# A graph layer's gathers and place transfers get semaphores of their own, one-hots are made two groups at a time, and five more groups leave the GpSimd queue

## The chip, the cores and the metric

The kernel runs on one core of one Trainium2 chip. The metric is the device time of one execution in microseconds (us); the lower the better. A kernel's time is the median of several executions. Engines are named as the profile names them: PE is TensorE, PEld its weight loads, DVE is VectorE, ACT is ScalarE, POOL is GpSimd, SP is SyncE. A name with a q behind it (DVEq, SPq, POOLq) is what the engine's instruction queue does beside its arithmetic: it waits for semaphores, loads registers and issues DMAs.

## What is computed

One layer of message passing on a graph of 12,500 nodes (128 numbers each) and 400,000 edges (32 numbers each), sorted by destination:

```python
h = relu(layernorm(x))
m = relu(concat(h[src], h[dst], edge_attr) @ w1 + b1) @ w2 + b2
agg = segment_sum(m, dst, 12500)
gi, gh = agg @ w_ih + b_ih, h @ w_hh + b_hh
r, z = sigmoid(i_r + h_r), sigmoid(i_z + h_z)
n = tanh(i_n + r * h_n)
out = x + (1 - z) * n + z * h
```

All of it is float32.

## The kernel before

**Once at the start.** The kernel normalizes the nodes, keeps h transposed in SBUF (`hT_all`), and writes A = h @ w1[0:128] to memory in HBM, one row of 512 bytes per node. The part for the destinations, B = h @ w1[128:256] + b1, is made in batches. Then the edges are worked through.

**Groups and units.** The 3125 tiles of 128 edges are cut into 391 groups `k` of 8 tiles (1024 edges; group 0 has 5 tiles). A group is two units `u` = 2k and 2k+1. Since the edges are sorted, a group touches at most 32 neighbouring nodes in each of its two halves.

**Work on a group.** For each group:

- `fetch` (L556) brings, for two groups at once, the destinations of the edges and the edge attributes into a buffer `L` with two DMAs on SP's queue, L563 and L566. There are three such buffers.
- `onehot_T` (L568, instruction at L575) turns the destinations in `L` into a one-hot matrix on VectorE, in place. With the rows of B in `RW` (`window_rows`, L602, SP) TensorE makes from it and from the attributes the part of the first product that doesn't depend on the source node (`pre`, L673).
- The row A[src] of every edge has to be added to that. There are four ways, and the dictionary `SPREAD` (L56) says how many groups go which way. **By GpSimd**: `gather` (L148) issues an indirect DMA per tile, eight per group (L156), into one of 11 buffers `G`; the first nine groups take raw rows of x, since A isn't there yet. **By SyncE**: 1024 single DMAs of 512 bytes each (L952) into `G_sp`. **By ScalarE or VectorE**: 1024 columns of `hT_all` are copied, one per edge, into a tile `HE_act` (L960) or, two edges an instruction, `HE_dve` (L967, put in order by L972); TensorE then multiplies them with w1[0:128] (L684).
- Where rows came by DMA, `add` adds them to `pre` and takes the relu in one instruction on VectorE (L701), into `RB`. For groups copied by ScalarE or VectorE the relu is one on ScalarE (L710).
- `onehot` (L606, instruction at L623) makes on VectorE a one-hot of the destinations with edges on the partitions, 128 by 256 per group, in one of six buffers `OH`. TensorE multiplies it with `RB` and sums up by node (`seg`, L724, after a zeroing product at L719).
- Each block of 14 groups ends in a `node` step: gates, tanh, output.

**Groups made by hand.** `one_by_one` (L934) is the work of ScalarE, VectorE and SyncE on such groups. The numbers of the rows are loaded from the tile `at` into registers of the engine (L945): 16 at a time on ScalarE, 32 on VectorE and SyncE. `run_jobs` (L988) strews the copies evenly over the units ahead of the group, in four phases of each unit. ScalarE starts on its first one at unit 4, VectorE at unit 14, SyncE at unit 24 (`START`), and each goes from one to the next.

**Order.** All instructions stand in the order in which the program writes them (`manual_schedule`), each engine has its own queue, and semaphores between them are set by the framework. A DMA counts up one of eight shared semaphores of its kind (one set for the hardware queue that SP uses, one for GpSimd's), by turns. An instruction that reads what eight DMAs brought waits for each of the eight, and a DMA whose turn falls on a semaphore waits until the DMA before it on that semaphore has landed. At unit `u` the loop runs `gathers(u)`, at even units `window_rows(k + 4)` and, every other group, `fetch`; then `stages(u)`: `onehot_T` or `onehot` for three groups ahead, `pre` three units ahead, `add` two units ahead; then `seg(u)`.

Of the kernel before, what the change touches and what calls it, by code (L numbers as in the profile page):

```python
# [9 lines left out]
F32 = mybir.dt.float32  # L10
F16 = mybir.dt.float16
I32 = mybir.dt.int32
# [17 lines left out]
V = 32  # L30
# [9 lines left out]
QP = 2  # L40
# [4 lines left out]
RAW = 9  # L45
GBUFS = 11
# [17 lines left out]
def tile_gnn(ctx: ExitStack, tc: tile.TileContext, x, src, srcT, dstT, dstP, eaT, eaP, w1, b1, w2T, b2,  # L64
             wih, bih, whh, bhh, out):
    nc = tc.nc
    ctx.enter_context(tc.manual_schedule())
    const = ctx.enter_context(tc.tile_pool(name="const", bufs=1))
# [12 lines left out]
    def tiles(k):  # L81
        return (0 if k == 0 else SUP0 + (k - 1) * PAIR, SUP0 + k * PAIR)


    def unit_tiles(u):
        k, h = divmod(u, 2)
        t0, t1 = tiles(k)
        return [(t0 + a * GRP + j, j, a) for j in (2 * h, 2 * h + 1) for a in range(2)
                if t0 + a * GRP + j < t1]

    mode, order = {}, {m: [] for m in SPREAD}
    for m, n in SPREAD.items():
# [49 lines left out]
    taker, ring = {}, []  # L142
    for k in range(NP):
        if k not in mode:
            taker[k] = ring[-GBUFS] if len(ring) >= GBUFS else -1
            ring.append(k)

    def gather(k):  # L148
        if k >= NP or k in mode:
            return  # L150
        G[k] = gp.tile([128, GRP, 2, D], F32, name="G")
        table = x if k < RAW else A
        for u in (2 * k, 2 * k + 1):
            for t, j, a in unit_tiles(u):
                c, i = divmod(t, CH)
                nc.gpsimd.indirect_dma_start(  # L156
                    out=G[k][:, j, a, :], out_offset=None, in_=table,
                    in_offset=bass.IndirectOffsetOnAxis(ap=src_i[c][:, i:i + 1], axis=0))

    for k in range(RAW):  # L160
        gather(k)
# [181 lines left out]
    with tc.tile_pool(name="pp", bufs=3) as pp:  # L343
# [50 lines left out]
        row = lambda v: v.rearrange("(o f) -> o f", o=1)  # L394
# [34 lines left out]
        for q in range(NC + 3):  # L429
            if q < NC:  # L430
                b, i0, c, e, P, n0 = chunk(q)
# [3 lines left out]
            if 1 <= q <= NC:  # L435
                b, i0, c, e, P, n0 = chunk(q - 1)
# [6 lines left out]
            if q >= 3:  # L443
                b, i0, c, e, P, n0 = chunk(q - 3)
# [3 lines left out]
            if q < NC:  # L448
                b, i0, c, e, P, n0 = chunk(q)
# [4 lines left out]
            if 1 <= q <= NC:  # L454
                b, i0, c, e, P, n0 = chunk(q - 1)
# [31 lines left out]
    dlast = p3.tile([128, BLOCKS[-1][1] + 128], F16, name="dlast", bufs=1)  # L487
# [63 lines left out]


    Ls, OH, RT, HE, SEG = ({} for _ in range(5))
    hand = {}

    def fetch(q):  # L556
        if q * QP >= NP:
            return
        n = min(QP, NP - q * QP)
        c = slice(q * QP * 512, (q * QP + n) * 512)  # L560
        Ls[q] = p3.tile([128, QP * 512], F32, name="L")
        p = dstP[:, c]
        nc.sync.dma_start(  # L563
            Ls[q].bitcast(I32)[:2 * V, :n * 512],
            bass.AP(tensor=p.tensor, offset=p.offset, ap=[list(p.ap[0]), [0, V], [1, n * 512]]))
        nc.sync.dma_start(Ls[q][2 * V:, :n * 512], eaP[:, c])  # L566

    def onehot_T(k):  # L568
        if k >= NP:
            return  # L570
        c = slice((k % QP) * 512, (k % QP + 1) * 512)
        o, i = Ls[k // QP][:2 * V, c], Ls[k // QP].bitcast(I32)[:2 * V, c]
        n = k - BLOCKS[-1][0]
        if n < 0:
            nc.vector.tensor_scalar(o, i, node_of[:, k:k + 1], None, op0=ALU.is_equal)  # L575
        else:
            nc.vector.tensor_scalar(o, i, node_of[:, k:k + 1], 0.0, op0=ALU.is_equal, op1=ALU.add,
                                    accum_out=dlast[:2 * V, n:n + 1])


    bases = {}
# [22 lines left out]
                                  "(p f) -> p f", p=V))  # L604

    def onehot(k):  # L606
        if k >= NP:
            return
        t0, t1 = tiles(k)
        OH[k] = OHB[k % len(OHB)]  # L610
        row = SEGB[((k - 3) // 2 + 1) % 2][:, 256:256 + V]
        for a in range(2) if k == 0 else (None,):
            if a is None:
                o, s = OH[k].rearrange("p j a v -> p a j v"), slice(t0, t1)
                d = dloc[:, s].rearrange("p (a j) -> p a j", a=2)[:, :, :, None]
                shape = [128, 2, GRP, V]
                i = row[:, None, None, :]
            else:
                e = min(t1, (a + 1) * GRP)
                o, d = OH[k][:, :e - a * GRP, a, :], dloc[:, a * GRP:e, None]  # L620
                shape = [128, e - a * GRP, V]
                i = row[:, None, :]
            nc.vector.tensor_tensor(o, d.to_broadcast(shape), i.to_broadcast(shape),  # L623
                                    op=ALU.is_equal)

    def unit(u):
        k, h = divmod(u, 2)
# [59 lines left out]
    def add(u):  # L687
        if u >= NU or u < 0:
            return
        k, h = divmod(u, 2)  # L690
        if h == 0 and k < NP - 1:
            return
        c = slice(0, PAIR) if k < NP - 1 else slice(GRP * h, GRP * h + GRP)
        o, p = RB[k % 2][:, c, :D], PP[k][:, c, :]
        if u in HE or k in hand:
            RT[u] = o, p
            HE.pop(u, None)
            HE.pop(u - 1, None)
            hand.pop(k, None)
        else:  # L700
            nc.vector._custom_dve(TENSOR_ADD_SAT, out=o, in0=p,  # L701
                                  in1=G[k].rearrange("p j a f -> p (j a) f")[:, c, :], s0=float("inf"), s1=0.0)
        if h == 1:
            PP.pop(k)
            G.pop(k, None)
# [9 lines left out]
    def seg(u):  # L715
        k, h = divmod(u, 2)
        p = SEGB[(k // 2) % 2]
        if h == 0 and k % 2 == 0:
            nc.tensor.matmul(p[:, :D + 1], zrow[:, :128], zrow[:, :D + 1], start=True, stop=False)  # L719
        l = unit_tiles(u)  # L720
        rest = l if h else l + unit_tiles(u + 1)
        for i, (t, j, a) in enumerate(l):
            r0 = 2 * V * (k % 2) + V * a
            nc.tensor.matmul(p[r0:r0 + V, :D + 1], OH[k][:, j, a, :],  # L724
                             RB[k % 2][:, 2 * j + a, :D + 1], start=False,
                             stop=all(b != a for _, _, b in rest[i + 1:]))

# [287 lines left out]
    for q in range(3):  # L1015
        fetch(q)
# [4 lines left out]
    def stages(u):  # L1021
        if u + 7 >= 0:
            raw_stats(u + 7)
        if u + 6 >= 0:
            raw_fin(u + 6)
            raw_h(u + 6)
        if u % 2 == 0:
            onehot_T(u // 2 + 3)
        elif u > -7:
            onehot(u // 2 + 3)  # L1030
        if u + 4 >= 0:
            raw_turn(u + 4)
        if u + 3 >= 0:
            pre(u + 3)
        if u + 2 >= 0:
            add(u + 2)
            relu(u + 2)
# [18 lines left out]
    for u in range(NU):  # L1056
        k, h = divmod(u, 2)
        gathers(u)
        if h == 0:
            window_rows(k + 4)  # L1060
            if k % QP == 0:
                fetch(k // QP + 3)
            if k and k == BLOCKS[block(k)][0]:
                nodes_left.append([node(block(k) - 1), 2 if k < BLOCKS[-1][0] else 1])
            if k % PLACE == 1:
                indices(k // PLACE + 2)
            if k % PLACE == 5:
# [23 lines left out]
        other(1)  # L1091
        other(2)
        seg(u)
        if u == 0:
            node_setup()
# [106 lines left out]
    f = nc.values_load(flag[0:1, 0:1], min_val=0, max_val=1)  # L1202
# [67 lines left out]
```

## Time and profile before

| | |
|---|---|
| time, median of 3 runs | 3404.46 us (3404.36 to 3407.26) |
| profiled execution, its own time | 3403.76 us |
| its span, first to last instruction | 3401.8 us |
| busy: PE / PEld / DVE | 71% / 46% / 65% |
| busy: ACT / POOL | 91% / 75% |
| granted TensorE clock, mean | 0.796 |
| mean DMA rate | 99 GB/s |
| groups gathered by POOL / by hand on ACT, DVE, SP | 334 / 28, 27, 2 |

The busy time counts arithmetic, and for POOL the making of indirect DMAs. Loading registers, waiting for semaphores and issuing DMAs is not counted as busy. "Idle before" a group of instructions is the idle time of the engine just ahead of them, with what ended it; "issue" means that nothing which the profile shows was waited for.

### The profile page before, as it was taken

What the parts mean: (1) busy time and instruction counts of PE and PEld (TensorE: products, weight loads), DVE (VectorE), ACT (ScalarE), POOL (GpSimd) and SP (SyncE); (2) the same over time, 40 slices, a digit from 0 to 9 for tenths busy, and PEclk for the clock granted to TensorE, in tenths of its full rate; (3) what the DMA queues carried; (4) which work ended last, traced back from release to release, by engine and by line L of the source; (5) the groups of instructions that cost most, each with busy time, mean ns of one, the idle gap of its engine ahead of it and who ended that gap; (6) DMA issues with size and microseconds to landing.
All of it is one profiled execution on the core that took longest, in us unless ns stands there. A gap on an engine that the chain in (4) does not pass through costs nothing. (4 is left out here: it accounts for less than half of the span.)

```text
span 3401.8 us, 88642 instructions
## 1 busy us (share of the span) xinstructions
PE 2417.4 (71%) x13113; PEld 1563.7 (46%) x13113; DVE 2225.1 (65%) x16468; ACT 3079.4 (91%) x29057; POOL 2566.1 (75%) x2678
## 2 busy tenths in 40 slices
PE   7567777777677767776777667676677767766767
PEld 7444444444445444544444444444444434444445
DVE  8556666666676666666666666666666666666665
ACT  7699999999999998999899988988988898898984
POOL 7777777777777777777777777777777777777776
PEclk9777887887887778777877877788777778777878
DMA  6434444434443333343434433443433334343332
GB/s 213 106 88 93 97 100 99 101 94 100 102 98 94 98 99 95 95 101 97 98 93 99 98 94 93 96 96 93 98 93 92 95 94 99 92 97 96 92 92 73
DMA packets 191316, 335.44 MB, mean 99 GB/s; under 512 B 66753, under 2 KB 112384, under 8 KB 190729
## 3 DMA queue, kind: packets, MB, share of 16 engines
q0 software_dynamic: 85408, 175.09, 23.0%
q1 hardware_dynamic: 105177, 154.58, 16.4%
q14 instruction: 478, 3.92, 0.4%
q8 instruction: 109, 1.79, 0.2%
q10 hardware_dynamic: 144, 0.07, 0.0%
HBM read 309.24 MB, written 20.24 MB: 97 GB/s over the span
## 5 line engine op out<-in xcount | busy, mean ns | idle before, releaser
L156 POOL DMA_INDIRECT G<-A,src_i x2600 | 2498.9, 961 | 796.2 <-issue 753.7
L960 ACT COPY HE_act<-hT_all 128x4 uint8 x28672 | 2886.8, 189 | 51.4 <-issue 27.0
L967 DVE SCALAR_TENSOR_TENSOR both<-hT_all 128x4 uint16 x13824 | 1173.4, 153 | 988.5 <-issue 980.7
L673 PE MATMUL pre<-RW,L 128*128 128x256 f32 x3128 | 1132.4, 488 | 229.8 <-DVE RB L701 220.6
L673 PEld LDWEIGHTS pre<-RW,L 128*128 128x128 f32 x3128 | 660.6, 236 | 506.1 <-DVE RB L701 234.0
L724 PE MATMUL seg<-RB,OH 128*32 128x129 f32 x6250 | 603.9, 324 | 380.0 <-DVE RB L701 349.7
L724 PEld LDWEIGHTS seg<-RB,OH 128*32 128x32 f32 x6250 | 333.1, 125 | 820.4 <-DVE RB L701 532.7
L701 DVE CUSTOM_DVE_ANT_0 RB<-pre,G 128x1024 f32<-128x1024 f32 (+1 forms) x326 | 394.5, 1210 | 62.7 <-DMA G<-A,src_i 49.2
L575 DVE TENSOR_SCALAR L<-L,node_of 64x512 f32<-64x512 int32 x382 | 186.7, 489 | 9.7 <-DMA L<-in_dstP 9.4
L719 PE MATMUL seg<-zrow 1*128 1x129 bf16 x196 | 45.3, 231 | 164.4 <-DVE OH L623 164.2
L623 DVE TENSOR_TENSOR OH<-dloc,seg 128x256 f32<-128x256 f16 (+1 forms) x392 | 159.5, 407 | 0.5 <-issue 0.5
L750 PE MATMUL nd<-spot,sums 128*128 128x40 f32 x782 | 116.6, 321 | 1.2 <-DVE sums L733 1.2
L750 PEld LDWEIGHTS nd<-spot,sums 128*128 128x128 f32 x782 | 112.4, 231 | 10.5 <-issue 9.0
L710 ACT ACTIVATE RB<-pre 128x1024 f32<-128x1024 f32 x64 | 65.0, 1015 | 52.4 <-PE pre L684 52.4
L809 ACT ACTIVATE gt<-nd 128x512 f32<-128x512 f32 (+2 forms) x28 | 16.4, 585 | 96.5 <-PE nd L803 96.5
L972 DVE COPY HE_dve<-both 128x512 uint8<-128x512 uint8 x216 | 96.6, 447 | 7.4
L684 PEld LDWEIGHTS pre<-w1a,HE_act 128*128 128x128 f32 x448 | 88.4, 245 | 11.6
L684 PEld LDWEIGHTS pre<-w1a,HE_dve 128*128 128x128 f32 x432 | 87.9, 252 | 12.1
L684 PE MATMUL pre<-w1a,HE_act 128*128 128x128 f32 x448 | 86.4, 327 | 0.0
L684 PE MATMUL pre<-w1a,HE_dve 128*128 128x128 f32 x432 | 85.1, 333 | 0.0
L156 POOL DMA_INDIRECT G<-in_x,src_i x69 | 65.9, 954 | 21.8 <-issue 20.7
L233 PE MATMUL nd<-w1b,hT_all 128*128 128x128 f32 x224 | 45.5, 346 | 43.3 <-DVE xb L835 43.3
(177 smaller groups left out, 1383.9 us busy)
## 6 DMA issues: line engine op xcount, KB each, us to landing
L<-in_dstP SPq DMA_DIRECT2D x195, 256.0 KB
L<-in_eaP SPq DMA_DIRECT2D x195, 256.0 KB
G<-A,src_i POOLq DMA_INDIRECT x2600
G_sp<-A SPq DMA_DIRECT2D x2048, 0.5 KB
RW<-B SPq DMA_DIRECT2D x782, 16.0 KB
xb<-in_x SPq DMA_DIRECT2D x26, 256.0 KB
out<-xb SPq DMA_DIRECT2D x26, 256.0 KB
xs<-in_x SPq DMA_DIRECT2D x11, 512.0 KB
```

The source lines that it names most:

```text
L156: nc.gpsimd.indirect_dma_start(out=G[k][:, j, a, :], out_offset=None, in_=table, in_offset=bass.IndirectOffsetOnAxis(ap=src_i[c][:, i:i + ...
L575: nc.vector.tensor_scalar(o, i, node_of[:, k:k + 1], None, op0=ALU.is_equal)
L623: nc.vector.tensor_tensor(o, d.to_broadcast(shape), i.to_broadcast(shape), op=ALU.is_equal)
L673: nc.tensor.matmul(p[:, 2 * i:2 * i + 2, :], Ls[k // QP][:, c0:c0 + 128], RW[k % 4], start=True, stop=not raw)
L684: nc.tensor.matmul(p[:, 2 * i + a, :], cols, w1a, start=False, stop=n + 1 == len(l) or l[n + 1][1] != j)
L701: nc.vector._custom_dve(TENSOR_ADD_SAT, out=o, in0=p, in1=G[k].rearrange("p j a f -> p (j a) f")[:, c, :], s0=float("inf"), s1=0.0)
L710: nc.scalar.activation(o, p, AF.Relu)
L724: nc.tensor.matmul(p[r0:r0 + V, :D + 1], OH[k][:, j, a, :], RB[k % 2][:, 2 * j + a, :D + 1], start=False, stop=all(b != a for _, _, b in r ...
L750: nc.tensor.matmul(p[:, bass.ds(offs[i], V + SHIFT)], sums[:, slot(b, i), :D], spot[:, i % 2, :], start=False, stop=i == len(offs) - 1)
L960: nc.scalar.copy(he[:, e * 4:e * 4 + 4], column(v))
L967: nc.vector.scalar_tensor_tensor(both[:, (e0 % PIECE + i) // 2, :], column(vals[i + 1]), 256.0, column(vals[i]), op0=ALU.mult, op1=ALU.add)
L972: nc.vector.tensor_copy(he[:, p0 * 4:(p0 + PIECE) * 4].rearrange("p (n c b) -> p n c b", c=2, b=4), both.bitcast(U8).rearrange("p n (b c) ...
```

## The change

The change has four parts.

1. **Gathers.** Eleven semaphores `filled`, one per buffer `G`. All gathers but those of the first nine groups and of the last one count up the semaphore of their buffer and take no turn on the shared ones. Ahead of the `add` stands one wait until all eight have landed.
2. **Places.** Three semaphores `landed`, one per buffer `L`. The two DMAs of `fetch` count up that of their buffer, and take no turn on the shared ones. VectorE waits for it once per buffer, ahead of the first `onehot_T`.
3. **One-hots.** `onehot` makes those of an even group and the one behind it in a single instruction, 128 by 512, in one of three buffers of double size. Groups 0 and 1 and the last stay single. The elements lie in the order of the tiles, half by half, and `seg` reads them so.
4. **Spread.** ScalarE 28 to 29 groups, VectorE 27 to 28, SyncE 2 to 5; so GpSimd gathers 329 and not 334.

```diff
-SPREAD = {"dve": 27, "act": 28, "sp": 2}
+SPREAD = {"dve": 28, "act": 29, "sp": 5}
...
+    filled = [tc.alloc_semaphore(f"filled{i}") for i in range(GBUFS)]
+    uses, goal = [0] * GBUFS, {}
     def gather(k):
...
+        i = ring.index(k) % GBUFS
+        if RAW <= k < NP - 1:
+            uses[i] += 1
+            goal[k] = filled[i], 16 * PAIR * uses[i]
...
-                nc.gpsimd.indirect_dma_start(
+                fetched = nc.gpsimd.indirect_dma_start(
...
+                if k in goal:
+                    fetched.then_inc(goal[k][0], 16)
+                    tc.no_tile_sem_insts.add(fetched.ins.name)
+                    tc.add_to_no_dep_group(f"rows{k}", fetched.ins)
...
-    OHB = [const.tile([128, GRP, 2, V], F32, name=f"OH{i}") for i in range(6)]
+    OHB = [const.tile([128, 2 * PAIR, V], F32, name=f"OH{i}") for i in range(3)]
...
+    landed = [tc.alloc_semaphore(f"landed{i}") for i in range(3)]
...
+            fetched.then_inc(landed[q % 3], 16)
+            tc.no_tile_sem_insts.add(fetched.ins.name)
+            tc.add_to_no_dep_group(f"places{q}", fetched.ins)
...
+        q = k // QP
+        if k % QP == 0:
+            nc.vector.wait_ge(landed[q % 3], 32 * (q // 3 + 1))
...
-        if k >= NP:
+        if k >= NP or (k % 2 and k > 1):
             return
+        o = OHB[(k // 2) % len(OHB)]
+        n = 2 if 1 < k < NP - 1 else 1
+        t0, t1 = tiles(k)[0], tiles(k + n - 1)[1]
...
+            nc.vector.tensor_tensor(p, dloc[:, e0:e1, None].to_broadcast(shape),
+                                    row[:, None, :].to_broadcast(shape), op=ALU.is_equal)
...
+            if k in goal:
+                nc.vector.wait_ge(*goal[k])
```

More of the change, by code (lines that the diff above doesn't have):

```diff
@@ L562, in fetch @@
         p = dstP[:, c]
[L563 to L566, printed above, removed]
+        for fetched in (
+                nc.sync.dma_start(
+                    Ls[q].bitcast(I32)[:2 * V, :n * 512],
+                    bass.AP(tensor=p.tensor, offset=p.offset, ap=[list(p.ap[0]), [0, V], [1, n * 512]])),
+                nc.sync.dma_start(Ls[q][2 * V:, :n * 512], eaP[:, c])):
+            fetched.then_inc(landed[q % 3], 16)
+            tc.no_tile_sem_insts.add(fetched.ins.name)
+            tc.add_to_no_dep_group(f"places{q}", fetched.ins)
     def onehot_T(k):
@@ L574, in onehot_T @@
         if n < 0:
-            nc.vector.tensor_scalar(o, i, node_of[:, k:k + 1], None, op0=ALU.is_equal)
+            made = nc.vector.tensor_scalar(o, i, node_of[:, k:k + 1], None, op0=ALU.is_equal)
         else:
-            nc.vector.tensor_scalar(o, i, node_of[:, k:k + 1], 0.0, op0=ALU.is_equal, op1=ALU.add,
-                                    accum_out=dlast[:2 * V, n:n + 1])
+            made = nc.vector.tensor_scalar(o, i, node_of[:, k:k + 1], 0.0, op0=ALU.is_equal, op1=ALU.add,
+                                           accum_out=dlast[:2 * V, n:n + 1])
+        tc.declare_no_dep(made.ins, group=f"places{q}", reason="behind the wait for the landing")
+        if k % QP == 0:
+            tc.declare_fence(made.ins, group=f"places{q}")
     bases = {}
@@ L606, in onehot @@
     def onehot(k):
-        if k >= NP:
+        if k >= NP or (k % 2 and k > 1):
             return
-        t0, t1 = tiles(k)
-        OH[k] = OHB[k % len(OHB)]
+        o = OHB[(k // 2) % len(OHB)]
         row = SEGB[((k - 3) // 2 + 1) % 2][:, 256:256 + V]
[L612 to L624, printed above, removed]
+        n = 2 if 1 < k < NP - 1 else 1
+        for i in range(n):
+            OH[k + i] = o[:, PAIR * ((k + i) % 2):PAIR * ((k + i) % 2) + PAIR, :]
+        t0, t1 = tiles(k)[0], tiles(k + n - 1)[1]
+        if k:
+            parts = ((o[:, PAIR * (k % 2):PAIR * (k % 2) + t1 - t0, :], t0, t1),)
+        else:
+            parts = tuple((OH[0][:, a * GRP:min(t1, (a + 1) * GRP), :], a * GRP, min(t1, (a + 1) * GRP))
+                          for a in range(2))
+        for p, e0, e1 in parts:
+            shape = [128, e1 - e0, V]
+            nc.vector.tensor_tensor(p, dloc[:, e0:e1, None].to_broadcast(shape),
+                                    row[:, None, :].to_broadcast(shape), op=ALU.is_equal)
     def unit(u):
@@ L700, in add @@
         else:
-            nc.vector._custom_dve(TENSOR_ADD_SAT, out=o, in0=p,
+            if k in goal:
+                nc.vector.wait_ge(*goal[k])
+            made = nc.vector._custom_dve(TENSOR_ADD_SAT, out=o, in0=p,
                                   in1=G[k].rearrange("p j a f -> p (j a) f")[:, c, :], s0=float("inf"), s1=0.0)
+            if k in goal:
+                tc.declare_no_dep(made.ins, group=f"rows{k}", reason="behind the wait for the landing")
+                tc.declare_fence(made.ins, group=f"rows{k}")
         if h == 1:
@@ L723, in seg @@
             r0 = 2 * V * (k % 2) + V * a
-            nc.tensor.matmul(p[r0:r0 + V, :D + 1], OH[k][:, j, a, :],
+            nc.tensor.matmul(p[r0:r0 + V, :D + 1], OH[k][:, a * GRP + j, :],
                              RB[k % 2][:, 2 * j + a, :D + 1], start=False,
```

## The prediction

> **What bounds the kernel now.** The page comes first: its span, and what POOL does.
>
> ```profile
> span 3401.8 us, 88642 instructions
> L156 POOL DMA_INDIRECT G<-A,src_i x2600 | 2498.9, 961 | 796.2 <-issue 753.7
> L156 POOL DMA_INDIRECT G<-in_x,src_i x69 | 65.9, 954 | 21.8 <-issue 20.7
> ```
>
> POOL is called 75% busy, but the two rows with the idle time before them make 2498.9 + 796.2 + 65.9 + 21.8 = 3382.8 us of a span of 3401.8. So a gather takes 3382.8 / 2669 = 1.267 us, pause included. The timeline of POOL, first and last rows, says what the pause is:
>
> ```profile
> 3.27 1.10 POOL L156 DMA_INDIRECT G<-in_x,src_i  x1 [1.10 <-DMA src_i<-in_srcT]
> 4.67 0.94 POOL L156 DMA_INDIRECT G<-in_x,src_i  x1 [0.31 <-issue]
> 5.92 0.94 POOL L156 DMA_INDIRECT G<-in_x,src_i  x1 [0.30 <-issue]
> ...
> 3382.70 0.94 POOL L156 DMA_INDIRECT G<-A,src_i  x1 [0.30 <-issue]
> 3383.95 0.94 POOL L156 DMA_INDIRECT G<-A,src_i  x1 [0.30 <-issue]
> ```
>
> The same 0.30 us stands before the second gather, whose shared semaphore no DMA has used yet, and before the last. It belongs to the instruction; no semaphore is waited for in it. POOL works without a hole from 3.27 to 3384.89, and 16.9 us later all is over.
>
> That isn't the whole bound. Next I counted gathers (first pair of rows) and adds (second pair) before and after 250 us, with the stretches' view held to L156 and to L701:
>
> ```profile
> 0.00:250.00 250.00, 185.24 (x194) 0.82 0.49 137
> 250.00:1600.00 1350.00, 1024.05 (x1066) 0.81 0.40 98
> ...
> 0.00:250.00 250.00, 7.27 (x6) 0.82 0.49 137
> 250.00:1600.00 1350.00, 172.19 (x142) 0.81 0.40 98
> ```
>
> At 250 us POOL has issued 194 gathers, 24.6 groups. Nine of them (raw rows) need no add, six are added: it leads by 9.6 groups, with 11 buffers. At 1600 us it is 157.9 groups, nine raw, 148 added: a lead of 0.9. So for half of the run VectorE catches up, and is itself the bound; from then on it meets POOL. The waits of VectorE in 250 to 1600, in 1700 to 3350 and over all (in this order) say the same:
>
> ```profile
> DVE both L967 <- issue: 413.5, 368, 2.6
> DVE RB L701 <- DMA G<-A,src_i: 1.3, 4, 0.6
> ...
> DVE RB L701 <- DMA G<-A,src_i: 38.1, 23, 3.7
> DVE xb L238 <- PE nd L233: 16.6, 4, 4.8
> DVE RB L701 <- PE pre L673: 8.7, 4, 2.9
> ...
> DVE both L967 <- issue: 980.7, 847, 2.8
> DVE RB L701 <- DMA G<-A,src_i: 49.2, 31, 3.7
> ```
>
> In the first stretch VectorE waits for nobody: the stretches' view has it busy for 915.91 of 1350 us, and 413.5 are "issue".
>
> ```profile
> 250.00:1600.00 1350.00, 993.62 (x5380) 631.28 (x5379) 915.91 (x6957) 1290.30 (x12575) 1024.05 (x1066) 0.81 0.40 98
> 1700.00:3350.00 1650.00, 1145.71 (x6180) 726.58 (x6181) 1058.83 (x7993) 1498.79 (x14423) 1252.55 (x1305) 0.78 0.39 95
> ```
>
> Three engines lie close together, then. **POOL** sets the end; **VectorE** would end at most 49.2 us sooner without the waits for gathers, 3352.6, and at least 3327.3 if a late VectorE met the 16.6 + 8.7 us of waits on PE no more. I take the middle, 3340. **ScalarE** (fourth figure) has 59.7 us idle in the first stretch and 151.2 in the second.
>
> **The change part by part.** *Gathers off POOL.* Five groups of eight at 1.267 us are 50.7 us. What is left per gather stays as it is, since the pause held no wait. POOL would end at 3334.2, and with the same 16.9 us of tail the span is 3351.1. That is the floor.
>
> *One more group on VectorE.* The groups by line of VectorE in 250 to 1600, with the one-hot and the nearest 128x512 instruction that also reads PSUM:
>
> ```profile
> L967 DVE SCALAR_TENSOR_TENSOR both<-hT_all 128x4 uint16 x6116 | 519.2, 153 | 419.7 <-issue 413.5 <-DMA G_sp<-A 5.2
> L701 DVE CUSTOM_DVE_ANT_0 RB<-pre,G 128x1024 f32<-128x1024 f32 x142 | 172.2, 1213 | 4.7 <-PE pre L673 2.9 <-DMA G<-A,src_i 1.3 <-issue 0.4
> L623 DVE TENSOR_TENSOR OH<-dloc,seg 128x256 f32<-128x256 f16 x166 | 67.8, 408 | 0.0
> L972 DVE COPY HE_dve<-both 128x512 uint8<-128x512 uint8 x96 | 43.1, 449 | 3.3
> L813 DVE TENSOR_TENSOR gt<-gt,misc 128x512 f32<-128x512 f32 x12 | 8.2, 680 | 0.1
> ```
>
> A group is 512 instructions of L967 at (519.2 + 413.5) / 6116 = 0.1525 us, 78.1, and eight copies of L972 at 0.449, 3.6: together 81.7 us more. Adds go from 328 to 326, 2.4 less; SyncE's three new groups are added as the gathered ones were.
>
> *One-hots.* 195 pairs become one instruction each. By the durations, two of 408 ns against one of about 680 save 0.136 us a pair. But such instructions overlap:
>
> ```profile
> 1518.67 0.41 DVE L623 TENSOR_TENSOR OH<-dloc,seg 128x256 f32<-128x256 f16 x1
> 1519.01 1.21 DVE L701 CUSTOM_DVE_ANT_0 RB<-pre,G 128x1024 f32<-128x1024 f32 x1
> ```
>
> The next one starts 0.34 us after the one-hot. So I count 0.34 twice against 0.68 - 0.07 = 0.61, about 0.07 a pair: 14 us less. The ends are 0 (512 elements cost two times 256) and 26.5.
>
> *Waits of VectorE.* What a line's own view lists on the queue:
>
> ```profile
> L701 DVEq EVENT_SEMAPHORE  x1358: 21/50/2846, 201.2 to 3386.5; - x194
> L575 DVEq EVENT_SEMAPHORE  x129: 21/21/21, 148.2 to 3301.6; - x129
> L945 DVEq TENSOR_LOAD <-at x864: 2095/2150/3239, 188.2 to 3336.5; - x173
> ```
>
> An add has about four waiting instructions ahead of it for its eight shared semaphores, 50 ns each (median). One per gathered group stays, so some 1010 go: 50.5 us of queue time. The waits of L575 grow from 129 to about 196, 1.4 us. Is queue time VectorE's time? The queue is served in order, and the load of 32 numbers (2.15 us) comes behind the waits. Of 864 loads, 847 end with VectorE idle ("issue", 847 times), so there the queue is the later one, and what stands ahead of the load counts. Where it has instructions enough queued, a wait is hidden. The ends are 0 and twice 50.5, if the pause behind a wait is as long as the wait (an estimate; no row shows it). I take 50.5.
>
> [...]
>
> VectorE's own end: 3340 + 81.7 - 2.4 - 14 - 50.5 + 1.4 = 3356.2. That is 5 us behind POOL's floor, and the later one counts.
>
> *ScalarE.* One more group; its groups by line in 250 to 1600:
>
> ```profile
> L960 ACT COPY HE_act<-hT_all 128x4 uint8 x12514 | 1251.7, 189 | 18.9 <-issue 8.5
> L710 ACT ACTIVATE RB<-pre 128x1024 f32<-128x1024 f32 x24 | 24.4, 1016 | 15.1 <-PE pre L684 15.1
> L809 ACT ACTIVATE gt<-nd 128x512 f32<-128x512 f32 x12 | 7.1, 592 | 21.8 <-PE nd L803 21.8
> ```
>
> 1024 copies at 0.100 us and two more relus at 1.0 are 104.4 us, over 3200 us 3.3%. It had 59.7 / 1350 = 4.4% idle where VectorE was the bound. So it just fits, hidden in idle time that it spent on PE's results. [...]
>
> *SyncE's queue.* Its waits, and rows of its timeline:
>
> ```profile
> SPq L952 <- DMA L<-in_dstP: 865.4, 150, 8.1
> SPq L563 <- PE pre L673: 233.9, 63, 14.1
> ...
> 1521.30 1.27 SPq L952 DMA_DIRECT2D G_sp<-A  x4
> 1522.74 0.81 SPq L602 DMA_DIRECT2D RW<-B  x2
> 1523.67 0.60 SPq L563 DMA_DIRECT2D L<-in_dstP  x1
> 1524.32 0.50 SPq L566 DMA_DIRECT2D L<-in_eaP  x1
> ```
>
> Before, single rows waited 865.4 us for transfers of places that held their shared semaphore; that goes. A single row costs 1.27 / 4 = 0.32 us, a group with its 32 loads (at 2.15, as VectorE's) 396, five 1980. The 782 transfers of L602 at 0.41 and 196 pairs of places at 1.15 add 546. In all 2526 of 3350: it fits, and the waits for PE (233.9) are room too. What is queued behind such rows are the next places and `RW`; places are asked for six groups ahead.
>
> *One-hots are made up to a group earlier, with the same memory.* That takes a buffer one group sooner from `seg`; PE, 71% busy, is the engine that waits for VectorE, so I count nothing. PE gets 16 more products at L684: nothing either, by the same cover.
>
> **The sum.** The later of 3351.1 and 3356.2, and the 2.0 us that the profiled execution lies over its span (3403.76 - 3401.8): 3358. That execution is 0.7 us under the median of the runs, which I leave aside.
>
> **The rivals.**
>
> *ScalarE binds.* If half of its idle 4.4% can't be filled, because gates wait for PE whenever they come, it lacks 3.3 + 2.2 - 4.4 = 1.1% of 3200, 35 us over POOL's floor: 3351 + 35 + 2 = 3388. For it: 91% busy. Against it: its idle time lies before L710 and L809, and a later ScalarE finds those results there.
>
> [...]
>
> *VectorE keeps up easily.* The waits save twice as much, POOL decides alone: 3353. For it: the pause behind waits.
>
> *The change doesn't do what it says:* gathers still wait on something shared, or SyncE falls behind with five groups and VectorE waits for rows instead. Then what POOL saves is lost again: about 3404.
>
> **Chances.** Forecast with POOL's floor in it, 3350 to 3375: 0.56. ScalarE or VectorE somewhat late, 3375 to 3397: 0.17. No change (waits hidden with the middle value, or lost again), within 0.2% of 3404, about what a measurement of this kernel can tell from no change: 0.07. Slower: 0.14. Below 3350, if a gather itself becomes cheaper than 1.267: 0.06. So faster 0.79, same 0.07, slower 0.14. The range is 3347 to 3405; what it leaves out is the slower cases and half of the last.
>
> **What would show it.** POOL without holes, 40 gathers fewer, 1.267 us each, ending near 3334: right for the first step. Semaphore instructions of L701's line down to about 350, and the time of L967 with its "issue" per instruction below 0.1525 us: right for the waits; unchanged: the waits were hidden. One-hots near 680 ns, 195 fewer. VectorE's waits for gathers shrink below 49.2 us if it is the bound, and grow if it keeps up. Waits of SP on places gone. The forecast fails if POOL shows waits for buffers (`RB` from VectorE), which means that VectorE fell back, or if ScalarE's idle time is gone and PE waits for it.

## The result, and the profile after

The changed kernel takes 4152.09 us (median of 4 runs, 4145.63 to 4160.77), against 3405.17 (4 runs, 3404.36 to 3407.26) for the kernel before beside it: 1.2196 times as long, 95% interval 1.2181 to 1.221. It is **22% slower**, and the forecast was 3358 with a range up to 3405.

The page of the changed kernel, its span and the groups that answer to those of before (GpSimd's gathers, TensorE's first product, VectorE's one-hots and pair copies):

```profile
span 4158.9 us, 94794 instructions
...
L163 POOL DMA_INDIRECT G<-A,src_i x2560 | 2453.2, 958 | 1508.9 <-DVE RB L724 766.8
...
L694 PE MATMUL pre<-RW,L 128*128 128x256 f32 x3128 | 1230.5, 523 | 1400.5 <-DMA RW<-B 1243.0
L993 DVE SCALAR_TENSOR_TENSOR both<-hT_all 128x4 uint16 x14336 | 1210.4, 156 | 1066.0 <-issue 1052.0
...
L594 DVE TENSOR_SCALAR L<-L,node_of 64x512 f32<-64x512 int32 x382 | 189.0, 495 | 679.1 <-DMA L<-in_eaP 679.1
...
L644 DVE TENSOR_TENSOR OH<-dloc,seg 128x512 f32<-128x512 f16 (+1 forms) x198 | 133.2, 673 | 0.0
```

Read the last column. The instructions are hardly dearer: a gather is 958 ns (961 before), a pair copy 156 ns (153). Among the rows shown only TensorE's first product takes clearly longer, 523 ns where it took 488, at a mean granted clock of 0.748 where it was 0.796. But every engine waits. TensorE waits 1243.0 us for `RW`, VectorE 679.1 us for the places, GpSimd 766.8 us for buffers that VectorE's adds give back. (GpSimd's wait for `RB` is the sign by which the prediction said that it would fail.) The first two are waits for DMAs, and both of those are issued by **SyncE**. So its queue is the place to look. What SyncE waits for (us in all, times, longest):

```profile
SPq L978 <- DMA G_sp<-A: 886.7, 172, 8.2
SPq L576 <- PE pre L694: 68.7, 28, 12.6
SPq L624 <- PE pre L694: 60.6, 16, 12.2
```

Before, the same kind of wait was 865.4 us under the name of the places; now it is 886.7 under the name of the single rows themselves. The name changed with the semaphore's other user, the time didn't. And SyncE waits little for TensorE to free the buffers of places (68.7 us at this line, 233.9 before): it is seldom early. The timeline of SyncE late in the run shows the wait itself:

```profile
4002.96 0.61 SPq L576 DMA_DIRECT2D L<-in_dstP  x1
4003.63 0.50 SPq L579 DMA_DIRECT2D L<-in_eaP  x1
4004.24 13.20 SPq L978 DMA_DIRECT2D G_sp<-A  x16
4017.53 0.82 SPq L624 DMA_DIRECT2D RW<-B  x2
4018.45 5.08 SPq L978 DMA_DIRECT2D G_sp<-A  x16
4023.78 0.41 SPq L865 DMA_DIRECT2D out<-xb  x1
4024.35 0.82 SPq L624 DMA_DIRECT2D RW<-B  x2
4025.22 0.59 SPq L576 DMA_DIRECT2D L<-in_dstP  x1
```

Sixteen rows cost 5.08 us (0.32 each) where nothing large is ahead, and 13.20 us right behind the two transfers of places, 512 KB in all. Taken from the trace row by row, the 13.20 us hold the rows themselves (5.2 us), a register load that falls among them (2.2), one stop of 5.3 us ahead of the ninth row, and a shorter one behind the load. The first eight rows find the eight shared semaphores free; the ninth has to wait until the row eight back has landed. By the semaphores' counts in the trace those eight rows land 7.0 to 8.0 us after their issue. Over the run the first eight rows behind places take 7.9 us to land (median), all others 1.4; and 172 of the 175 stops of over 0.5 us ahead of a row stand ahead of the ninth row behind a transfer of places. The waits for rows last 5.2 us on average (886.7 / 172), and one comes with nearly every transfer of places, that is, once per two groups. Behind it on the same queue stand `RW` and the next places, which TensorE and VectorE need.

**The queue's sum.** Counted in the trace from 250 to 4050 us, SyncE issues places for 180 pairs of groups, one pair per 21.1 us, and 5074 rows, 28 per pair. Its waits add up to 1009.5 us there, 5.6 per pair, 4.9 of them (877.2 us) for rows. The other 15.5 us are work of the queue: 28 rows at 0.32 to 0.34 make about 9.4, register loads 1.9 (342.2 us), four `RW` 1.9, places 1.2, the rest single instructions and gaps. The floor that was forecast, 3351 us for 195.5 pairs, is 17.1 per pair. So the queue's work fits and its work with the waits does not, and 195.5 x 21.1 = 4125 us is nearly the whole span.

### The profile page after: what moved, and what is told of

Read it like the earlier page. It is cut to its first block, busy times and chain, and to the rows that moved or that the text cites. A ratio compares the mean times of both kernels' runs of the same rounds, so it can differ in the third digit from the quotient of the medians.

```text
span 4158.9 us, 94794 instructions
## 1 busy us (share of the span) xinstructions
PE 2538.2 (61%) x13145; PEld 1614.1 (39%) x13145; DVE 2260.0 (54%) x16792; ACT 3191.8 (77%) x30083; POOL 2520.3 (61%) x2638
## 5 line engine op out<-in xcount | busy, mean ns | idle before, releaser
L163 POOL DMA_INDIRECT G<-A,src_i x2560 | 2453.2, 958 | 1508.9 <-DVE RB L724 766.8
L986 ACT COPY HE_act<-hT_all 128x4 uint8 x29696 | 2992.6, 189 | 55.8 <-issue 28.0
L694 PE MATMUL pre<-RW,L 128*128 128x256 f32 x3128 | 1230.5, 523 | 1400.5 <-DMA RW<-B 1243.0
L993 DVE SCALAR_TENSOR_TENSOR both<-hT_all 128x4 uint16 x14336 | 1210.4, 156 | 1066.0 <-issue 1052.0
L694 PEld LDWEIGHTS pre<-RW,L 128*128 128x128 f32 x3128 | 717.1, 256 | 1713.7 <-issue 1345.5
L750 PE MATMUL seg<-RB,OH 128*32 128x129 f32 x6250 | 623.8, 332 | 92.5 <-DVE RB L724 71.7
L594 DVE TENSOR_SCALAR L<-L,node_of 64x512 f32<-64x512 int32 x382 | 189.0, 495 | 679.1 <-DMA L<-in_eaP 679.1
L724 DVE CUSTOM_DVE_ANT_0 RB<-pre,G 128x1024 f32<-128x1024 f32 x321 | 390.0, 1215 | 29.6 <-PE pre L694 28.8
L644 DVE TENSOR_TENSOR OH<-dloc,seg 128x512 f32<-128x512 f16 (+1 forms) x198 | 133.2, 673 | 0.0
L825 PE MATMUL nd<-DEG,brow 34*128 34x512 f32 (+2 forms) x112 | 75.5, 760 | 4.2 <-ACT gt L835 3.7
L829 PE MATMUL nd<-TOT,w2ih 128*128 128x512 f32 (+2 forms) x112 | 71.0, 721 | 0.0
```

The source lines that it names most:

```text
L163: fetched = nc.gpsimd.indirect_dma_start(out=G[k][:, j, a, :], out_offset=None, in_=table, in_offset=bass.IndirectOffsetOnAxis(ap=src_i[c] ...
L594: made = nc.vector.tensor_scalar(o, i, node_of[:, k:k + 1], None, op0=ALU.is_equal)
L644: nc.vector.tensor_tensor(p, dloc[:, e0:e1, None].to_broadcast(shape), row[:, None, :].to_broadcast(shape), op=ALU.is_equal)
L694: nc.tensor.matmul(p[:, 2 * i:2 * i + 2, :], Ls[k // QP][:, c0:c0 + 128], RW[k % 4], start=True, stop=not raw)
L724: made = nc.vector._custom_dve(TENSOR_ADD_SAT, out=o, in0=p, in1=G[k].rearrange("p j a f -> p (j a) f")[:, c, :], s0=float("inf"), s1=0.0)
L750: nc.tensor.matmul(p[r0:r0 + V, :D + 1], OH[k][:, a * GRP + j, :], RB[k % 2][:, 2 * j + a, :D + 1], start=False, stop=all(b != a for _, _, ...
```

## The experiments

**Theories.** Theory 1: the single rows take turns on shared semaphores and so wait for a transfer of places ahead of them; the spread's five groups turn that wait, which SyncE had slack for, into the pace of the kernel. The other numbered theories of the first experiments look for the loss elsewhere, where semaphores of the rows' own would not mend it. The lettered theories of the later ones are about VectorE, once SyncE is mended. Nine of the eighteen runs were made where the kernel before itself took about 5700 us, and could not answer; they stand last. The others are single runs on four chips, each beside a run of the kernel before, which took 3396.92 to 3403.94 us there; so a few us between runs of different chips mean little.

### Rows with semaphores of their own (e6)

```diff
+    single = [tc.alloc_semaphore(f"single{i}") for i in range(8)]
+    singles = {k: n + 1 for n, k in enumerate(order["sp"])}
...
+            if k in singles:
+                for s in single:
+                    nc.vector.wait_ge(s, 16 * PAIR * 128 // len(single) * singles[k])
...
-                    nc.sync.dma_start(...)
+                    fetched = nc.sync.dma_start(...)
+                    fetched.then_inc(single[e % len(single)], 16)
+                    tc.no_tile_sem_insts.add(fetched.ins.name)
+                    tc.add_to_no_dep_group(f"rows{k}", fetched.ins)
```

> The changed kernel whose single rows count up eight semaphores of their own, on a chip where the kernel before takes about 3404 us. Theory 1 (rows wait for the row eight before them, which lands only behind the places): 3350 to 3370 us. Theory 2 (the issuing of 5120 rows fills the queue): over 3900. Theory 3 (the semaphores of their own or the double one-hots cost): over 4000.

Measured: **3418.38 us**, before 3401.69. The time is 734 us shorter than that of the changed kernel. Waits of SyncE and, below, its timeline at a transfer of places:

```profile
SPq L578 <- PE pre L696: 153.9, 44, 14.1
SPq L626 <- PE pre L696: 92.9, 24, 12.3
```

```profile
1524.94 0.58 SPq L578 DMA_DIRECT2D L<-in_dstP  x1
1525.58 0.55 SPq L581 DMA_DIRECT2D L<-in_eaP  x1
1526.24 5.29 SPq L983 DMA_DIRECT2D G_sp<-A  x16
```

Sixteen rows behind the places now take 5.29 us, and SyncE is early again: it waits for TensorE. The same number of rows is issued on the same queue, so the number of rows is not the cause. Theory 1 stands and its rivals fall. But the kernel is still no faster than before, with VectorE's and GpSimd's waits as follows:

```profile
DVE both L1001 <- issue: 1013.3, 814, 2.9
...
DVE L L596 <- DMA L<-in_eaP: 13.0, 3, 10.6
```

```profile
POOL G L165 <- issue: 781.3, 2562, 0.3
POOL G L165 <- DVE RB L729: 5.2, 15, 0.7
```

VectorE waits for no gather at all, and GpSimd's last gather starts at 3327.9 us, 88.7 before the end of the span (3416.6): VectorE sets the end. So the expected 3350 to 3370 was missed too; this is taken up from e13 on.

### Places cut to a 32nd (e12)

The rows stay on the shared semaphores, and the transfer ahead of them is made small. From the fourth pair of groups on only 32 of 1024 columns come; that part of the data is left out.

```diff
+    LB = [p3.tile([128, QP * 512], F32, name=f"L{i}", bufs=1) for i in range(3)]
...
-        Ls[q] = p3.tile([128, QP * 512], F32, name="L")
+        Ls[q] = LB[q % 3]
...
+        w = n * 512 if q < 3 else 32
...
-                    Ls[q].bitcast(I32)[:2 * V, :n * 512], ...[1, n * 512]
-                nc.sync.dma_start(Ls[q][2 * V:, :n * 512], eaP[:, c])
+                    Ls[q].bitcast(I32)[:2 * V, :w], ...[1, w]
+                nc.sync.dma_start(Ls[q][2 * V:, :w], eaP[:, c.start:c.start + w])
```

> The changed kernel, 29, 28 and 5 groups, its single rows on the shared semaphores, but from the fourth pair of groups on only 32 of the 1024 columns of places and attributes are transferred, 8 KB a DMA for 256 (what stands in the three buffers is stale, so the result is that of other edges). The two DMAs are still issued. Theory 1 (a row lands only behind the places ahead of it, so the ninth row behind them waits): the rows' waits of 886.7 us mostly go and VectorE is the bound, 3400 to 3440 us. Theory 2 (the issuing of rows fills the queue by itself): about 4150.

Measured: **3417.70 us**, before 3396.92. Its largest waits of SyncE, and sixteen rows behind places in its timeline:

```profile
SPq L626 <- PE pre L696: 301.2, 67, 13.8
SPq L626 <- DMA B<-xb: 53.8, 25, 3.8
```

```profile
1532.48 0.60 SPq L578 DMA_DIRECT2D L<-in_dstP  x1
1533.12 0.56 SPq L581 DMA_DIRECT2D L<-in_eaP  x1
1533.82 5.17 SPq L980 DMA_DIRECT2D G_sp<-A  x16
```

No wait for a row is left, on shared semaphores, with the same count of DMAs, and the first eight rows behind places now land after 1.4 us (median) as all others do. So the two halves of the cause are shown, each by taking it alone away: a large transfer ahead, and a semaphore whose turn comes round while it is still under way (in the stretch shown of the changed kernel, counts of the places issued from 4002.96 us go on until 4012.79). Either cure gives about the same time, 3418.

Rows of 512 bytes land 7.9 us after their issue behind 512 KB, and 1.4 us after it elsewhere (medians in the changed kernel). What holds them back there, no run here takes apart.

### The spread alone, on the kernel before (e15)

```diff
-SPREAD = {"dve": 27, "act": 28, "sp": 2}
+SPREAD = {"dve": 28, "act": 29, "sp": 5}
```

> The kernel before with the changed spread alone (29, 28, 5), shared semaphores, single one-hots. Theory 1 (rows wait behind the places just as much; the transfers of places only lent the semaphore its name): 4100 to 4400 us. If the semaphores of their own or the double one-hots are what costs: about 3420.

Measured: **4304.67 us**, before 3396.92. So the new semaphores are not what made the kernel slow; the spread does it alone. The waits of SyncE:

```profile
SPq L952 <- DMA L<-in_dstP: 940.2, 175, 7.7
SPq L952 <- DMA L<-in_eaP: 98.0, 173, 1.4
```

Here the rows share their semaphores with the places, and wait 1038.2 us instead of 886.7. The 151.5 us of difference are nearly found again in the end: the span is 4302.8 and not 4158.9, 143.9 later. That is what one expects of a queue that sets the pace, though the two kernels differ in more than these waits.

### The change with two groups on SyncE (e18)

```diff
-SPREAD = {"dve": 28, "act": 29, "sp": 5}
+SPREAD = {"dve": 28, "act": 29, "sp": 2}
```

> The changed kernel as it is, with SyncE's groups back at 2 (ScalarE 29, VectorE 28). Theory 1: SyncE's queue has room again for rows that wait behind places, and VectorE with 28 groups is the bound as in the mended kernel: about 3415 us. If VectorE weren't the bound, GpSimd's end with 332 groups: 3384.

Measured: **3404.36 us**, before 3403.94. Its waits of SyncE:

```profile
SPq L978 <- DMA G_sp<-A: 505.1, 94, 7.7
SPq L624 <- DMA G_sp<-A: 375.7, 70, 7.8
SPq L576 <- PE pre L694: 364.5, 94, 14.0
```

The waits for rows are as large as ever, 505.1 + 375.7 = 880.8 us, and the time stays at that of before, because SyncE has 364.5 us and more to spare behind them. The same 880 us are free with 2 groups and set the time with 5. The measured time lies between the two expected ones. GpSimd's last gather ends at 3369.8 us, 32.8 before the end, and VectorE waits for none, so VectorE is the bound, some 11 us earlier than was expected.

### VectorE: what the gathers' own semaphores save (e13)

From here on the rows have their own semaphores (e6), so that SyncE no longer sets the pace. This run puts the gathers back on the shared ones:

```diff
-        if RAW <= k < NP - 1:
+        if False:
             uses[i] += 1
```

> The changed kernel with single rows on semaphores of their own (3418 us, VectorE the bound), and the gathers back on the eight shared semaphores, so each add has its waiting instructions again. Theory A (these waits are on VectorE's path): 3418 + 50 = 3468 us. Theory B (hidden): 3418.

Measured: **3476.21 us**, 57.8 more than e6 (62.6 more if each is first set against the kernel before on its chip: 79.3 and 16.7 us over it). The waiting instructions at the add, from that line's own view, in e13 and then in e6:

```profile
L729 DVEq EVENT_SEMAPHORE  x1326: 21/50/5689, 203.8 to 3454.4; - x190
```

```profile
L729 DVEq EVENT_SEMAPHORE  x50: 21/50/50, 201.8 to 3396.7; - x50
```

1276 waits of a median of 50 ns would be 63.8 us; 57.8 came, 45 ns each. VectorE waits for no gather in either run. Most of the difference is idle time at register loads, 1013.3 us in e6 and in e13:

```profile
DVE both L1001 <- issue: 1053.7, 883, 2.9
```

So queue time of waits is VectorE's time in this kernel, as the prediction took it, 45 ns for each.

### VectorE: single one-hots (e14)

e6 with `onehot` and its buffers as in the kernel before.

```diff
-        if k >= NP or (k % 2 and k > 1):
+        if k >= NP:
             return
...
```

> The changed kernel with single rows on semaphores of their own (3418 us, VectorE the bound, 28 groups on it), and the one-hots single again, one group an instruction in six buffers. If the double one-hots save what the forecast says (14 us): 3432. Theory C (a double one-hot leaves every other pair of register loads without work to hide behind, so that it costs VectorE more than the overlap it saves): 3360 to 3405.

Measured: **3422.02 us**, 3.6 more than e6 (8.4 if each is set against the kernel before on its chip); the forecast had 14. Between single runs on two chips that difference is hardly told from chance, but the rows show where the time went. The groups of VectorE from 250 to 1600 us, in e6 and then in e14:

```profile
L1001 DVE SCALAR_TENSOR_TENSOR both<-hT_all 128x4 uint16 x6148 | 519.7, 156 | 425.8 <-issue 423.5 <-DMA RW<-B 1.6
...
L646 DVE TENSOR_TENSOR OH<-dloc,seg 128x512 f32<-128x512 f16 x80 | 54.2, 678 | 0.0
```

```profile
L1002 DVE SCALAR_TENSOR_TENSOR both<-hT_all 128x4 uint16 x6135 | 520.2, 153 | 418.4 <-issue 411.5 <-DMA RW<-B 3.6
...
L647 DVE TENSOR_TENSOR OH<-dloc,seg 128x256 f32<-128x256 f16 x161 | 65.8, 408 | 0.0
```

With double instructions (e6) the one-hots get 11.6 us cheaper in this stretch, and the idle time marked "issue" gets 12.0 longer. So what the engine saves comes back as idle time at the copies. My reading, which no run tries apart, is that the engine then waits for the next load of registers, which stands behind as much on the queue as ever. The double one-hots didn't make VectorE late, and hardly helped it.

### VectorE: 27 groups again (e11 and its repeat e17)

```diff
-SPREAD = {"dve": 28, "act": 29, "sp": 5}
+SPREAD = {"dve": 27, "act": 29, "sp": 5}
```

on top of e6.

> Once more the changed kernel with single rows on semaphores of their own, ScalarE 29, VectorE 27, SyncE 5, on a chip where the kernel before takes about 3404 us. With 28 groups on VectorE it took 3418 us and VectorE was the bound. One group less takes 81.7 us off VectorE, and GpSimd gathers 330: 3402 - 4 x 8 x 1.267 + 2 = 3363 us if GpSimd is the bound again; 3400 or more if SyncE's queue or ScalarE is.

> The version with single rows on semaphores of their own and 29, 27 and 5 groups, a second time (3368.6 us beside 3399.3 before): 3364 to 3373 us.

Measured: **3368.62** us (before 3399.26) and **3380.49** (before 3403.94). Both are shorter than the kernel before beside them, by 0.9% and 0.7%, and than the changed kernel; they are two single runs on two chips. The repeat missed its expected 3364 to 3373. The two lie 12 us apart, and that is the gathers: they are busy for 2469.1 us in e11 and 2482.0 in e17, 961 and 967 ns each. So terms of about 10 us between single runs are not told from chance. In e11 GpSimd is the bound again; its waits and its gathers:

```profile
POOL G L165 <- issue: 783.2, 2568, 0.3
POOL G L165 <- DVE both L1001: 8.8, 29, 0.3
POOL G L165 <- DVE RB L729: 3.7, 11, 0.6
```

Its last gather starts at 3345.6 us, 21.1 before the end (3366.7). ScalarE's 29 groups fit.

### VectorE's own end with 27 groups (e16)

To separate VectorE's end before the change from the price of the 28th group: 27 groups, single one-hots, gathers on shared semaphores, rows and places on their own (the diffs of e13, e14 and e11 together on e6).

> SyncE's single rows and the places on semaphores of their own, gathers on the shared ones, single one-hots, 29, 27 and 5 groups: VectorE has the work and the waits of the kernel before, and GpSimd four groups less (end about 3363). Theory D (VectorE's own end before was not 3340 but nearly the end itself, because what it waited for gathers would otherwise have been idle time at register loads): from e13 and e14, 3476 + 4 - 82 = 3398 us. Theory E (its own end was 3327 to 3353, and the 28th group costs VectorE well over 81.7 us): GpSimd is the bound, 3363 to 3372 us.

Measured: **3390.39 us**, before 3403.94; span 3388.6. The waits of VectorE:

```profile
DVE both L1002 <- issue: 976.4, 849, 2.7
DVE L L596 <- DMA L<-in_eaP: 26.8, 7, 10.8
...
DVE gt L845 <- ACT gt L841: 10.6, 5, 3.6
```

It waits for no gather worth listing, so the end is VectorE's, but 37.4 us are waits for late places and for ScalarE, of which the kernel before had 10.8 (9.4 and 1.4). The result lies between the two expectations. It doesn't settle them.

### Nine runs that tell nothing of the question

Runs e1 to e5 and e7 to e10 were made where the kernel before itself took 5666.6 to 5718.85 us. (The record has e1 to e4 and e11 on the same chip number, with 5718.85 and 3399.26 us for the kernel before, so it isn't shown to belong to a chip.) They are told once, together: e1 (the change with 2 groups on SyncE), e2, e5 (e6's edit), e3, e10 (the spread alone), e4 (4 groups on SyncE), e7 (e11's edit), e8 (the change with the spread of before), e9 (the gathers' semaphores alone).

> The changed kernel with SyncE's groups back at 2 (ScalarE 29, VectorE 28), all else as changed. Theory 1 (SyncE's queue is the bound: each single row waits on its shared semaphore for the row eight before it, and rows asked for behind a pair of places land only after the places, so 5 groups fill the queue): SyncE has room again, GpSimd gathers 332 groups and is the bound, 3402 - 2 x 8 x 1.267 + 2 = 3384 us. Theory 2 (the mere issuing of 5120 rows fills the queue): also about 3384. Theory 3 (the semaphores of their own or the double one-hots are what costs): stays over 4000.

> The changed kernel, 29, 28 and 5 groups, and the 1024 single rows of SyncE's groups count up eight semaphores of their own as well, so no row waits for the row eight before it. Theory 1: the waits of the rows (886.7 us) go, SyncE needs about 3000 us, and the time falls to that of the original forecast, 3350 to 3370. Theory 2: rows cost the same issue time, the time stays over 3900. Theory 3: stays over 4000.

> The kernel before, shared semaphores and single one-hots, with the changed spread alone (ScalarE 29, VectorE 28, SyncE 5). Theory 1: rows wait behind the places just as much, since the transfers of places only lent the semaphore its name: 4100 to 4400 us. Theory 2: about 4150. Theory 3: about 3400.

> The changed kernel with 4 groups on SyncE (29 and 28 on the others). Theory 1: for two groups of edges (17.1 us at the pace before) SyncE has 22.5 rows at 0.32, 1.5 of loads, 4.3 of other transfers and the wait of about 5.9 behind the places, 18.9 us, times 195.5: about 3700 us. Theory 2 (issue time alone, with 5 groups at 21.2 us of which 11 are rows): 18.8 us, about the same. Theory 3: stays over 4000.

> Once more the changed kernel whose single rows count up eight semaphores of their own (the first time ScalarE, VectorE and PE sat idle between single instructions in the kernel before too, so that nothing of SyncE's queue could be told). Theory 1 (rows wait for the row eight before them, which lands only behind the places): 3350 to 3370 us where the kernel before takes about 3404. Theory 2 (the issuing of 5120 rows fills the queue): over 3900. Theory 3 (the semaphores of their own or the double one-hots cost): over 4000.

> The changed kernel with single rows on semaphores of their own, ScalarE 29, SyncE 5, and VectorE back at 27 groups. With SyncE's queue mended the kernel took 3418 us and VectorE never waited for a gather: VectorE is the bound there. One group less takes 81.7 us off VectorE, GpSimd gathers 330 groups: 3402 - 4 x 8 x 1.267 + 2 = 3363 us if GpSimd is the bound again, which both theories on VectorE's waits give; if SyncE's queue or ScalarE (29 groups) is the bound, 3400 or more.

> The changed kernel with the spread of before (28, 27, 2): semaphores of their own and double one-hots alone. GpSimd gathers as many groups as before, so about 3404 us, and what VectorE saves shows in the stretch from 250 to 1600 us, where it was the bound and made 166 groups at 8.13 us each. Theory A (the waits removed were on VectorE's path, 50.5 us over the run, and the double one-hots save 14): 7.97 us a group, 169 groups. Theory B (the waits were hidden behind queued work): only the one-hots save, 8.10 us a group, 167. If semaphores of their own cost by themselves: over 4000 us.

> The kernel before with one part of the change: the gathers count up semaphores of their buffers. About 3404 us. Theory A: 8.00 us a group between 250 and 1600 us, 169 groups. Theory B: 8.13, 166 groups as before.

> Once more the kernel before with the changed spread alone (29, 28, 5), shared semaphores, single one-hots. Theory 1 (rows wait behind the places just as much; the transfers of places only lent the semaphore its name): 4100 to 4400 us. If the semaphores of their own or the double one-hots are what costs: about 3420.

Measured, in us: e1 5739.47, e2 5792.58, e3 5717.7, e4 5776.91 (before 5718.85); e5 5787.75 (before 5706.73); e7 5814.15, e8 5691.76, e9 5653.26, e10 5689.24 (before 5666.6). None answers to its expectation: everything is bound by something else there. ScalarE's timeline in e1:

```profile
2018.74 0.29 ACT L986 COPY HE_act<-hT_all 128x4 uint8 x2 [0.40 <-issue]
2019.47 0.19 ACT L986 COPY HE_act<-hT_all 128x4 uint8 x1 [0.44 <-issue]
2020.19 0.19 ACT L986 COPY HE_act<-hT_all 128x4 uint8 x1 [0.53 <-issue]
2020.90 0.19 ACT L986 COPY HE_act<-hT_all 128x4 uint8 x1 [0.52 <-issue]
```

A copy lasts 0.19 us as ever, but they come in ones and twos, 0.71 us apart. VectorE's pair copies come thinly in e1 too; GpSimd's gathers keep their 0.94 us with 0.30 between. The granted clock is 0.669. The loss that this study is about doesn't appear there: the spread alone, 26.7% slower in e15, made no difference here (e3; 0.4% in e10), though SyncE's rows wait 352.2 us in e3 under the name of the places. That such waits find room between instructions so far apart is my reading, which no run tries. Why the instructions came so slowly is open.

## Why the prediction was wrong, step by step

**SyncE's queue: this step failed.** The prediction said of the 865.4 us of waits "that goes", and "In all 2526 of 3350: it fits". So its sum for SyncE's queue had no term for waits. It read the name of the wait, `L<-in_dstP`, as its cause: a semaphore that places hold. The name is only that of the last DMA on the semaphore. With the places on semaphores of their own the rows wait for each other's landing, which the places delay just the same (886.7 us; e6 and e12). The issue times were about right, 0.32 to 0.34 us a row and 2.14 us a load. The queue's work without waits is some 2914 us over the run by the trace, and not 2526; about 220 of that are other transfers and loads, which the sum left out. It would still have fitted in 3350: at 15.5 us per two groups it is under the 17.1 of the floor. What was missing is the waits, 5.6 us per two groups, 4.9 of them for rows.

**The rival "SyncE falls behind"** had part of the mechanism in its words (VectorE came to wait for places, 679.1 us, and for rows only 10.6), and a price that was no price: about 3404, "what POOL saves is lost again". A queue that is over full sets the pace of all; its price is its sum, 21.1 us per two groups times 195.5, and it has no reason to stop at the time of before. The range of the forecast ended at 3405.

**Cover of places and `RW`.** The prediction let late places be covered by asking six groups ahead. An engine that is behind on average uses up any lead: in the changed kernel TensorE waited 1243.0 us for `RW` and VectorE 679.1 us for places.

**GpSimd's floor: right**, seen once SyncE is mended. 40 gathers fewer, still 0.94 us each with 0.30 before it; the last one of e6 ends at 3328.8, forecast 3334.2.

**ScalarE fits: right.** In e11 29 groups end with GpSimd the bound.

**VectorE's end: wrong by 60 us**, and with SyncE mended this alone leaves the kernel 0.5% slower than before (e6, 3418.38 beside 3401.69). Forecast 3356.2, measured span 3416.6. By terms:

- The waits save 57.8 (e13), forecast 50.5: right in kind. In size two errors offset each other: 1276 waits of 45 ns went, and not 1010 of 50. The high end of that term, 101, supposed a pause behind each wait as long as the wait. The trace of the kernel before has such a pause (the waits of one add last 50 ns and start 98 ns apart, median of 1015), and yet 45 ns came for each.
- Double one-hots save 3.5 by the spans of e14 and e6 (3420.1 and 3416.6; 8.4 by the other reckoning), forecast 14: by these single runs mis-sized. The instruction got cheaper as forecast (0.14 us a pair by its duration), and the time came back as idle time.
- The rest is VectorE's own end and the price of the 28th group. Forecast 3340 + 81.7 - 2.4 + 1.4 = 3420.7; measured, e13's span (3474.4) and the 3.5: 3477.9. That is 57 us more, the term that failed. Some of it may come from the three new groups of SyncE, since e18, with two, ends 14 us before e6; that is hardly over the 12 us between e11 and e17. e16 bounds VectorE's own end from above, at 3388.6; less the 26.6 us of waits that it has more than the kernel before, that is about 3362 (an estimate), not 3340. By e16 as it stands, own end has 49 of the 57 us and the group the rest; the waits in it and the 12 us between equal runs forbid to lean on that. So how the 57 us divide between own end and group stays open.

One suspect is that 49.2 us of waits for gathers were taken for slack that would vanish, where idle time at register loads would have taken their place. In the kernel before, VectorE's idle time at a register load was about 1.09 us on average from 250 to 1600 us and 1.17 from 1700 to 3300, taken from the trace instruction by instruction; in e6, without any wait for gathers, it is 1.10 and 1.15. So the idle time at loads is larger in the second half even without gathers to wait for. This was not tried apart.

## What to carry to other kernels

The name on a DMA wait says whose count is awaited, not what delays it (here 865.4 us under the name of the places, and 886.7 under that of the rows once the places had semaphores of their own): ask what was issued just ahead on the same queue, and if small transfers share a few semaphores by turns behind a large one, give them semaphores of their own before adding more of them (4152 us became 3418 here). A wait that costs nothing is a statement on slack, so sum up the queue with its waits in it before more work goes there; once the sum passes the period of the loop, the price is the whole excess, in every round (21.1 us per two groups here, where the forecast had 17.1). And where an engine is nearly the bound, its end without the waits that you see is not its end minus those waits: measure it by a run in which the other bound is gone.

## What the runs showed of the hardware beyond that

- A row of 512 bytes costs SyncE 0.32 us to issue. Issued right behind 512 KB on the same queue it landed 7.9 us after its issue (median over the first eight rows behind places in the changed kernel, by the semaphores' counts), elsewhere 1.4 us after it. Where eight semaphores go round, the ninth such row stops the queue, for 5.2 us on average, and not at all when the 512 KB are cut to a 32nd (e12).
- A waiting instruction on VectorE's queue cost 45 ns of VectorE's time where the queue is the later one (57.8 us by 1276, e13 against e6), close to its own median of 50 ns.
- Beside nine of the runs the kernel before took about 5700 us instead of 3400. In e1 ScalarE's copies came in ones and twos about 0.71 us apart, each as long as elsewhere (0.19 us), while GpSimd's gathers kept their pace.
